# Post-norm attention and gated FFN layer on one core: the count of wide weights one block later, and the output normalisations of blocks 12 and 13 in other places

## The chip, the cores and the metric

The kernel runs on one core of a Trainium2 chip. A core has five engines that work side by side, each through its own queue in order: TensorE (PE, with its weight loads as PEld) does the matrix products, VectorE (DVE) and ScalarE (ACT) work on elements, GpSimd (POOL) does element work on SBUF, and SyncE (SP) issues most transfers. Products go to PSUM, which this kernel uses as eight banks of 128 x 512 float32. The metric is the time on the device in microseconds (us), the median over runs; lower is better.

## The reference

The input `x` has 4 x 2048 tokens of 256 features. The layer is attention in chunks of 32 tokens, with a decay mask and no softmax, then a gated FFN whose weights are integers of -127 to 127 times 1/127; each is followed by a layer norm over the sum with its input.

```python
Q = x @ W_q.T ; K = x @ W_k.T ; V = x @ W_v.T
mask = where(diff >= 0, decay ** diff, 0)              # within chunks of 32 tokens
O = ((Q K^T) * mask) @ V                               # chunk by chunk
x = layernorm(x + sigmoid(x @ W_g.T) * O @ W_o.T + x)
h = silu(x @ wg.T) * (x @ wu.T)                        # 768 hidden features
x = layernorm(x + h @ wd.T)
```

## The kernel before

**Tiles and precision.** The 8192 tokens are 16 blocks of 512 (`NB`, numbered 0 to 15). A block is held either with tokens on partitions (four groups of 128 tokens, `NG`) or with features on partitions. The FFN's products are exact to about float32: the integer weights are stored as `hi` (fp32r) and `lo` (f16), and each activation is split in two likewise, as the rounded part `hi` and the rest `lo`. ScalarE's copy makes `u_hi` from `u` (L757), GpSimd subtracts to make `u_lo` (L758).

**Products of the FFN.** `ffn_up` (L722) goes over chunks of 128 hidden features, six (`KH`) to a block. A chunk takes two banks, `pg` for the gate and `pu` for the other factor, with eight products. Then ScalarE makes the Sigmoid `s` of `pg` (L741), VectorE multiplies `s` by `pg` (L743), which frees the gate's bank, then `pu` by `s` (L755), which frees the other. `ffn_down` (L764) multiplies the six `u_hi` and six `u_lo` by `fd` for each of the four token groups (`fdn`, L625; even groups take the `hi` parts first), and VectorE adds the residual (L772) and takes the moments (L307, L308).

**Attention of a block** has a scores product (`ps`, L578), masked by VectorE (L589), a values product (`po`, L599), multiplied by the gate to give `goT` (L606), and an output product. Most blocks do the products for v, y, the gate and the output by a scheme with seven half-size products (`seven`, L439), in two halves: the first four, then `others`. For block 15 `attn_out` (L640) does the output directly (`pa`) and a whole layer norm on VectorE and ScalarE.

**The main loop** (L834) runs over b = 0 to 13. Pass b does the FFN of block b, the attention of block n = b + 2 from its scores on, and the first attention products of m = b + 3, which exist (`more`) up to b = 12. Blocks 14 and 15 have their FFN after the loop (L913 on), interleaved, with block 15 in two halves of 256 columns.

**Layer norms in the loop** are spread: VectorE's moments, then a root on ScalarE (`root`, L311), a reciprocal on VectorE and three small operations on GpSimd (`scale_and_shift`, L348), and four scalings on ScalarE, one for each group (`normalize`, L361), after which the block is stored by SP (L784). The root needs another activation table than the Sigmoids; after the roots the loop executes a Sigmoid of one column (`table`, L885), so that the table for Sigmoids is loaded at that place.

**Order.** The program is laid out by a framework that may issue an instruction earlier than it is written, when it thinks its inputs ready, and that puts in the waits. `keep_in_program_order` pins an instruction behind the one written just before it on the same engine; `in_turn` does that always, `in_steady_turn` only while `steady` is true (L842, passes 1 to 12), `free` never. An instruction that isn't pinned may be placed ahead of a pinned one. The SP queue carries, in every pass, 16 transfers that finish the transposition of `h` (`move_h`, L683; `split_h`, L706, then makes `hT_hi` on ScalarE and `hT_lo` on GpSimd).

**The count of wide weights.** The exact scheme holds only for integers up to 128 in size. `look_up` (L260) takes the largest size in each of nine pieces of the weights on VectorE, five before the loop and four in pass 0, after the values. `count_wide` (L272), right behind it in pass 0, compares them (`wide`, L275), adds over partitions with a product by ones (`pw`, L279), and makes an integer on VectorE. It is read at the very end, where a block for wide weights runs if the count isn't zero.

**Around the change.** In pass b the scalings of block b - 2 (`r_before`) stand after the values. In pass 13 the root of block 12 stands after `split_h` of block 14, and behind `ffn_down` come the root of 13 and then, for blocks 12 and 13, `scale_and_shift`, four scalings and the store (L899 to L907). Then the FFN of 14 begins (L918).

Of the kernel before, what the change touches and what calls it, by code (L numbers as in the profile page):

```python
# [51 lines left out]
AF = mybir.ActivationFunctionType  # L52
ALU = mybir.AluOpType
# [5 lines left out]
TB = 512  # L59
NG = TB // P  # L60
# [11 lines left out]
def kernel(  # L72
# [187 lines left out]
    def look_up(which):  # L260
        pieces = [piece for pieces in ffn_int for piece in pieces]
        for i in which:
            reduced = nc.vector.tensor_reduce(
                top[:, i : i + 1],
                pieces[i].rearrange("p k n -> p (k n)"),
                mybir.AxisListType.X,
                ALU.max,
                apply_absolute_value=True,
            )
            tc.keep_in_program_order(reduced)  # L270

    def count_wide():  # L272

        wide = const.tile([P, top.shape[1]], F32, tag="wide", name="wide")
        nc.vector.tensor_scalar(wide, top, EXACT, None, ALU.is_gt)  # L275
        ones = const.tile([P, 1], F32, tag="ones", name="ones")
        nc.vector.memset(ones, 1.0)
        pw = bank("pw")
        nc.tensor.matmul(pw[:1, : top.shape[1]], lhsT=ones, rhs=wide, start=True, stop=True)  # L279
        count = const.tile([1, 1], F32, tag="count", name="count")  # L280
        nc.vector.tensor_reduce(count, pw[:1, : top.shape[1]], mybir.AxisListType.X, ALU.add)
        n_wide = const.tile([1, 1], I32, tag="n_wide", name="n_wide")
        nc.vector.tensor_copy(n_wide, count)
        return n_wide

    def in_turn(ins):
        tc.keep_in_program_order(ins)
# [70 lines left out]
        nc.gpsimd.tensor_tensor(shift, mv[:, :, 0], minus, ALU.mult)  # L358
        return scale, shift

    def normalize(r, scale, shift):  # L361
        for g in range(NG):
            in_turn(
                nc.scalar.activation(  # L364
                    r[:, g, :],
                    r[:, g, :],
                    AF.Identity,
                    bias=shift[:, g : g + 1],
                    scale=scale[:, g : g + 1],
                )  # L370
            )
# [137 lines left out]
    def split_y(b, x_sums):  # L509
        yT = work.tile([P, KD, TB], F32, tag="yT", name=f"yT_{b}")  # L510
        return yT, seven(f"y_{b}", feature_major(w_sums["m"], x_sums), by_features(yT))
# [125 lines left out]
    def flat(t, gs):  # L637
        return t[:, gs, :].rearrange("p g d -> p (g d)")

    def attn_out(b, goT, up=H_UP):  # L640
        xn = xns.pop(b)
        r = norm.tile([P, NG, D], F32, tag="h", name=f"h_{b}")

        def residual(gs, pb):
            nc.vector.tensor_tensor(flat(r, gs), pb, flat(xn, gs), ALU.add)

        project_back(b, (chunked(goT),), (chunked(wo),), residual, "pa")
        layer_norm(r, f"a{b}", on_r=HALF, on_dst=up)
        return r
# [69 lines left out]
        return hi, lo  # L719


    def ffn_up(b, hT, uT, chunks, cols=slice(0, TB), held=False):  # L722

        n = cols.stop - cols.start
        for hc in chunks:
            pg = bank(f"fg_{b}_{hc}_{cols.start}")[:, :n]
            pu = bank(f"fu_{b}_{hc}_{cols.start}")[:, :n]

            kinds = (0, 1) if hc % 2 == 0 else (1, 0)
            for kind in kinds:  # L730
                for pb, w in ((pg, fg), (pu, fu)):
                    for dc in range(KD):
                        nc.tensor.matmul(  # L733
                            pb,
                            lhsT=w[kind][:, dc, hc * P : (hc + 1) * P],
                            rhs=hT[kind][:, dc, cols],
                            start=(kind == kinds[0] and dc == 0),
                            stop=(kind == kinds[1] and dc == KD - 1),
                        )
            s = work.tile([P, n], F32, tag="s", name=f"s_{b}_{hc}")  # L740
            nc.scalar.activation(s, pg, AF.Sigmoid, scale=SCALE / H_UP)  # L741

            gated = nc.vector.scalar_tensor_tensor(  # L743
                s, pg, U_UP / H_UP**2, s, ALU.mult, ALU.mult
            )
            in_steady_turn(gated)
            if len(uT[0]) == hc:
                for kind, dtype, tiles in zip(("hi", "lo"), (F32R, F16), uT):
                    tiles.append(
                        acts.tile([P, TB], dtype, tag=f"u_{kind}", name=f"u_{kind}_{b}_{hc}")  # L750
                    )

            def multiply(hc=hc, pu=pu, s=s):
                u = work.tile([P, n], F32, tag="u", name=f"u_{b}_{hc}")
                in_steady_turn(nc.vector.tensor_tensor(u, pu, s, ALU.mult))  # L755
                hi, lo = uT[0][hc][:, cols], uT[1][hc][:, cols]
                nc.scalar.copy(hi, u)  # L757
                nc.gpsimd.tensor_tensor(lo, u, hi.bitcast(F32), ALU.subtract)  # L758

            if held:  # L760
                return multiply
            multiply()
# [68 lines left out]

    scales_h = scales_out = r_out = None
    table = const.tile([P, 1], F32, tag="table", name="table")
    for b in range(NB - 2):  # L834
        n = b + 2
        m = b + 3
        more = m < NB
        xns[n] = load_xn(n)
        hT = hTs.pop(b)
        uT = [], []  # L840
        yT, v, sg = ahead
        steady = 0 < b < NB - 3  # L842
        if b:
            normalize(hs[b + 1], *scales_h)
        moving = move_h(b + 1, hs[b + 1])
        ffn_up(b, hT, uT, range(0, 1))
        if b == 0:
            g_rest()
            x_sums = token_sums(xTs[m], f"x_{m}")
        ffn_up(b, hT, uT, range(1, 2))  # L850
        sT = attn_scores(n, yT)
        if m + 1 < NB:
            xTs[m + 1] = load_xT(m + 1)
        ffn_up(b, hT, uT, range(2, 3))
        if more:
            v_next, v_rest = split_v(m, x_sums)
        multiply = ffn_up(b, hT, uT, range(3, 4), held=True)
        if more:
            v_rest()
        multiply()  # L860
        goT = attn_values(n, sT, v, sg)
        if scales_out is not None:
            normalize(r_before, *scales_out)
            store(b - 2, r_before)
        if b == 0:
            look_up(range(5, n_pieces))
            n_wide = count_wide()
        if more:
            go_sums = token_sums(goT, f"go_{n}")
            y_next, y_rest = split_y(m, x_sums)  # L870
        ffn_up(b, hT, uT, range(4, KH))
        r_before = r_out
        if more:
            y_rest()
            sg_next, g_rest = split_gate(m, x_sums)
            hs[n], out_rest = split_out(n, go_sums)
            g_rest()
            mv_h = out_rest()
            ahead = y_next, v_next, sg_next
            hTs[b + 1] = split_h(b + 1, moving)  # L880
            std_h = root_in_turn(mv_h, of_h, f"h_{b}")
            if b:
                mv_before, std_before = mv_out, root_in_turn(mv_out, of_out, f"out_{b}")

            in_turn(nc.scalar.activation(table, eps, AF.Sigmoid))  # L885
            if m + 1 < NB:

                x_sums = token_sums(xTs[m + 1], f"x_{m + 1}", in_turn)

            def between():  # L890
                return scale_and_shift(mv_h, std_h, of_h, f"h_{b}")

            r_out, mv_out, scales_h = ffn_down(b, uT, hs.pop(b), between)
            if b:
                scales_out = scale_and_shift(mv_before, std_before, of_out, f"out_{b}")
        else:
            hs[n] = attn_out(n, goT, 1)
            hTs[b + 1] = split_h(b + 1, moving)
            mv_before, std_before = mv_out, root_in_turn(mv_out, of_out, f"out_{b}")  # L899
            r_out, mv_out, _ = ffn_down(b, uT, hs.pop(b))  # L900
            std = root_in_turn(mv_out, of_out, f"last_{b}")
            for block, r, mv, of_r in (
                (b - 1, r_before, mv_before, std_before),
                (b, r_out, mv_out, std),
            ):
                normalize(r, *scale_and_shift(mv, of_r, of_out, f"f{block}"))
                store(block, r)  # L907

# [4 lines left out]
    cols = [slice(i * per * P, (i + 1) * per * P) for i in range(2)]  # L915
    uT_last = [], []
    uT = [], []
    ffn_up(last - 1, hTs[last - 1], uT, half[0])  # L918
    hTs[last] = transpose_h(last, hs[last], 1)
    ffn_up(last - 1, hTs[last - 1], uT, half[1])  # L920
    early = half[0]
    ffn_up(last, hTs[last], uT_last, early, cols[0])
# [211 lines left out]
```

## Time and profile before

| | |
|---|---|
| median of 3 runs | 540.35 us (540.34 to 541.08) |
| profiled execution | 540.2 us |
| its span, first to last instruction | 538.4 us |
| mean granted TensorE clock | 0.986 |
| one pass of the loop, fdn to fdn (115.02 to 146.62) | 31.6 us |
| pass 13, fdn of 12 ends to fdn of 13 ends | 468.0 to 490.6 |
| last fdn product of block 15 ends | 529.2 |

All times in the text are of the profiled execution, counted from the start of its span, unless they are called a median. About 1.8 us of the profiled execution lie outside its span. "Granted clock" is the share of full speed at which TensorE was let run. A line of the chain of waits has a start, a length, and what ran; a line of waits names the waiting engine, tile and line, then what ended the wait, then the total, the number and the longest wait in us. In a line of the order of time, the text in brackets at the end is the idle time before it and what ended that. "xN" is a number of instructions. A line of a stretch has the stretch and its length, the busy time of PE, PEld, DVE, ACT and POOL with the number of instructions, the granted clock, the DMA engines' busy share and GB/s.

### The profile page before, as it was taken

What the parts mean: (1) busy time and instruction counts of PE and PEld (TensorE: products, weight loads), DVE (VectorE), ACT (ScalarE), POOL (GpSimd) and SP (SyncE); (2) the same over time, 40 slices, a digit from 0 to 9 for tenths busy, and PEclk for the clock granted to TensorE, in tenths of its full rate; (3) what the DMA queues carried; (4) which work ended last, traced back from release to release, by engine and by line L of the source; (5) the groups of instructions that cost most, each with busy time, mean ns of one, the idle gap of its engine ahead of it and who ended that gap; (6) DMA issues with size and microseconds to landing.
All of it is one profiled execution on the core that took longest, in us unless ns stands there. A gap on an engine that the chain in (4) does not pass through costs nothing.

```text
span 538.4 us, 10518 instructions
## 1 busy us (share of the span) xinstructions
PE 521.3 (97%) x3642; PEld 423.1 (79%) x3642; DVE 388.9 (72%) x979; ACT 320.3 (59%) x638; POOL 330.4 (61%) x450
## 2 busy tenths in 40 slices
PE   8999799999999999999999999999999999999793
PEld 5588678797878879787887978788897878877592
DVE  4679748678686867868676786867677686777684
ACT  2374436466665656566575656666565675757753
POOL 5231736684857768486676848667684766643553
PEclk9999979999999999999999999999999999999898
DMA  7631301211313132131312312131231312020102
GB/s 252 184 112 39 79 0 44 77 40 37 91 52 99 43 83 73 34 89 55 101 41 61 98 33 87 52 105 41 51 108 31 88 53 68 1 78 15 64 1 82
DMA packets 43176, 36.90 MB, mean 69 GB/s; under 512 B 4720, under 2 KB 39024, under 8 KB 43120
## 3 DMA queue, kind: packets, MB, share of 16 engines
q1 hardware_dynamic: 41712, 34.88, 22.1%
q10 hardware_dynamic: 1376, 1.31, 0.7%
q8 instruction: 30, 0.49, 0.4%
q14 instruction: 26, 0.21, 0.1%
q0 software_dynamic: 32, 0.00, 0.0%
HBM read 20.45 MB, written 8.39 MB: 54 GB/s over the span
## 4 chain that ended last, share of the span: by engine, by line
PE 95%; DVE 2%; ACT 2%; issue 0%
PE fg L733 16%; PE fu L733 16%; PE fdn L625 15%; PE p_y L409 8%; PE p_v L427 8%; PE p_g L409 8%; PE p_o L427 8%; PE po L599 5%; PE ps L578 3%; PE pa L625 2%; PE py L539 1%; PE pv L558 1%; PE pg L523 1%; PE pi L178 1%; ACT r L364 1%; PE fdn L977 1%
## 5 line engine op out<-in xcount | busy, mean ns | idle before, releaser
L758 POOL TENSOR_TENSOR u_lo<-u,u_hi 128x512 f16<-128x512 f32 (+1 forms) x102 | 123.6, 1214 | 128.8 <-ACT u_hi L757 126.9
L757 ACT CAST u_hi<-u 128x512 fp32r<-128x512 f32 (+1 forms) x102 | 60.6, 594 | 67.4 <-DVE u L755 67.1
L743 DVE SCALAR_TENSOR_TENSOR s<-fg,s 128x512 f32<-128x512 f32 (+1 forms) x102 | 66.7, 656 | 43.4 <-ACT s L741 43.4
L741 ACT ACTIVATE s<-fg 128x512 f32<-128x512 f32 (+1 forms) x102 | 56.7, 569 | 40.2 <-PE fg L733 40.0
L733 PE MATMUL fg<-hT_hi,fg_hi 128*128 128x512 f32 (+1 forms) x204 | 75.7, 453 | 2.8 <-DVE s L743 2.8
L755 DVE TENSOR_TENSOR u<-fu,s 128x512 f32<-128x512 f32 (+1 forms) x102 | 66.9, 658 | 10.7 <-POOL u_lo L758 1.1
L733 PE MATMUL fu<-hT_hi,fu_hi 128*128 128x512 f32 (+1 forms) x204 | 61.6, 383 | 0.0
L733 PE MATMUL fg<-hT_lo,fg_lo 128*128 128x512 f16 (+1 forms) x204 | 59.2, 372 | 0.0
L733 PE MATMUL fu<-hT_lo,fu_lo 128*128 128x512 f16 (+1 forms) x204 | 59.0, 371 | 0.0
L625 PE MATMUL fdn<-fd_hi,u_hi 128*128 128x256 f32 x360 | 52.9, 289 | 0.0
L733 PEld LDWEIGHTS fg<-hT_hi,fg_hi 128*128 128x128 f32 x204 | 36.1, 192 | 12.0 <-DVE s L743 3.2
L625 PEld LDWEIGHTS fdn<-fd_hi,u_hi 128*128 128x128 f32 x360 | 45.1, 189 | 0.4
L625 PE MATMUL fdn<-fd_lo,u_lo 128*128 128x256 f16 x360 | 44.6, 273 | 0.0
L733 PEld LDWEIGHTS fu<-hT_hi,fu_hi 128*128 128x128 f32 x204 | 37.8, 190 | 8.5 <-DVE s L743 0.3
L364 ACT ACTIVATE h<-h,shift_h,scale_h 128x256 f32<-128x256 f32 x52 | 27.0, 592 | 22.6 <-POOL shift_h L358 22.6
L733 PEld LDWEIGHTS <-fu_lo 128*128 128x128 f16 x204 | 20.0, 98 | 21.8 <-issue 0.6
L716 POOL TENSOR_TENSOR hT_lo<-hT,hT_hi 128x512 f16<-128x512 f32 x28 | 35.3, 1280 | 2.3 <-ACT hT_hi L715 2.3
L625 PEld LDWEIGHTS <-u_lo 128*128 128x128 f16 x360 | 32.7, 98 | 4.7 <-POOL u_lo L758 0.2
L772 DVE SCALAR_TENSOR_TENSOR r<-fdn,h 128x512 f32<-128x512 f32 x30 | 20.7, 691 | 20.4 <-PE fdn L625 20.4
L733 PEld LDWEIGHTS <-fg_lo 128*128 128x128 f16 x204 | 16.0, 99 | 20.7 <-issue 13.2
L599 PE MATMUL po<-sT,v 128*128 128x128 f32 x256 | 31.2, 275 | 0.0
L599 PEld LDWEIGHTS po<-sT,v 128*128 128x128 f32 x256 | 30.0, 192 | 0.6 <-issue 0.5
(192 smaller groups left out, 1134.4 us busy)
## 6 DMA issues: line engine op xcount, KB each, us to landing
x<-in_x_dram SPq DMA_DIRECT2D x16, 512.0 KB, 3.6
xT<-in_xT_dram SPq DMA_DIRECT2D x15, 512.0 KB, 4.3
hT<-sq SPq DMA_DIRECT2D x224, 32.0 KB, 1.9
out_dram<-r SPq DMA_DIRECT2D x14, 512.0 KB, 4.8
fg_int<-in_ffn_gT_dram SPq DMA_DIRECT2D x3, 256.0 KB, 8.3
fu_int<-in_ffn_uT_dram SPq DMA_DIRECT2D x3, 256.0 KB, 7.0
fd_int<-in_ffn_dT_dram SPq DMA_DIRECT2D x3, 256.0 KB, 6.0
out_dram<-r SPq DMA_DIRECT2D x6, 128.0 KB, 3.1
```

The source lines that it names most:

```text
L364: nc.scalar.activation(r[:, g, :], r[:, g, :], AF.Identity, bias=shift[:, g : g + 1], scale=scale[:, g : g + 1],)
L409: nc.tensor.matmul(pb, lhsT=a[i - 1], rhs=b[i - 1], start=first, stop=True, skip_group_check=True,)
L427: nc.tensor.matmul(pb[:, g * P : (g + 1) * P], lhsT=b[i - 1][:, g * P : (g + 1) * P], rhs=a[i - 1], start=first and g == 0, stop=True, ski ...
L599: nc.tensor.matmul(po[:, cols], lhsT=v[:, g, dc * P : (dc + 1) * P], rhs=sT[:, cols], start=True, stop=True,)
L625: nc.tensor.matmul(pb[:, j * D : (j + 1) * D], lhsT=part[:, g * P : (g + 1) * P], rhs=w, start=(i == 0), stop=(i == len(terms) - 1),)
L716: nc.gpsimd.tensor_tensor(in_order[1], whole, in_order[0].bitcast(F32), ALU.subtract)
L733: nc.tensor.matmul(pb, lhsT=w[kind][:, dc, hc * P : (hc + 1) * P], rhs=hT[kind][:, dc, cols], start=(kind == kinds[0] and dc == 0), stop=( ...
L741: nc.scalar.activation(s, pg, AF.Sigmoid, scale=SCALE / H_UP)
L743: gated = nc.vector.scalar_tensor_tensor(s, pg, U_UP / H_UP**2, s, ALU.mult, ALU.mult)
L755: in_steady_turn(nc.vector.tensor_tensor(u, pu, s, ALU.mult))
L757: nc.scalar.copy(hi, u)
L758: nc.gpsimd.tensor_tensor(lo, u, hi.bitcast(F32), ALU.subtract)
```

## The change

- `count_wide` is called in pass 1 instead of pass 0. `look_up` stays in pass 0.
- `steady` holds in pass 13 too, and ends after the loop; the residual of `attn_out` is added under `in_steady_turn`.
- In pass 13 the scalings of block 11 and its store stand between chunks 2 and 3 rather than after the values.
- In pass 13 the root of block 12, the return to the Sigmoids' table (now the function `back_to_sigmoids`) and `scale_and_shift` stand after the values, ahead of chunks 4 and 5; the scalings of 12 and its store stand after these chunks.
- The root of 13 stays behind `ffn_down`; the return to the Sigmoids' table follows it. Its scalings move into the FFN of block 14, two groups after chunk 1 and two after the transposition of block 15. The first Sigmoid of block 14 is pinned.

```diff
-    def normalize(r, scale, shift):
-        for g in range(NG):
+    def normalize(r, scale, shift, groups=range(NG)):
+        for g in groups:
...
-            nc.vector.tensor_tensor(flat(r, gs), pb, flat(xn, gs), ALU.add)
+            in_steady_turn(nc.vector.tensor_tensor(flat(r, gs), pb, flat(xn, gs), ALU.add))
...
-    def ffn_up(b, hT, uT, chunks, cols=slice(0, TB), held=False):
+    def ffn_up(b, hT, uT, chunks, cols=slice(0, TB), held=False, order=free):
...
-            nc.scalar.activation(s, pg, AF.Sigmoid, scale=SCALE / H_UP)
+            order(nc.scalar.activation(s, pg, AF.Sigmoid, scale=SCALE / H_UP))
...
+    def back_to_sigmoids():
+
+        in_turn(nc.scalar.activation(table, eps, AF.Sigmoid))
+
...
-        steady = 0 < b < NB - 3
+        steady = b > 0
...
         ffn_up(b, hT, uT, range(2, 3))
+        if not more:
+            normalize(r_before, *scales_out)
+            store(b - 2, r_before)
...
-        if scales_out is not None:
+        if scales_out is not None and more:
             normalize(r_before, *scales_out)
             store(b - 2, r_before)
         if b == 0:
             look_up(range(5, n_pieces))
+        if b == 1:
             n_wide = count_wide()
         if more:
             go_sums = token_sums(goT, f"go_{n}")
             y_next, y_rest = split_y(m, x_sums)
+        else:
+            std_out = root_in_turn(mv_out, of_out, f"out_{b}")
+            back_to_sigmoids()
+            scales_out = scale_and_shift(mv_out, std_out, of_out, f"out_{b}")
         ffn_up(b, hT, uT, range(4, KH))
...
-            in_turn(nc.scalar.activation(table, eps, AF.Sigmoid))
+            back_to_sigmoids()
...
         else:
+            normalize(r_before, *scales_out)
+            store(b - 1, r_before)
             hs[n] = attn_out(n, goT, 1)
             hTs[b + 1] = split_h(b + 1, moving)
-            mv_before, std_before = mv_out, root_in_turn(mv_out, of_out, f"out_{b}")
             r_out, mv_out, _ = ffn_down(b, uT, hs.pop(b))
-            std = root_in_turn(mv_out, of_out, f"last_{b}")
-            for block, r, mv, of_r in (
-                (b - 1, r_before, mv_before, std_before),
-                (b, r_out, mv_out, std),
-            ):
-                normalize(r, *scale_and_shift(mv, of_r, of_out, f"f{block}"))
-                store(block, r)
+            std_out = root_in_turn(mv_out, of_out, f"last_{b}")
+            back_to_sigmoids()
+            scales_out = scale_and_shift(mv_out, std_out, of_out, f"last_{b}")
+    steady = False
...
-    ffn_up(last - 1, hTs[last - 1], uT, half[0])
+    ffn_up(last - 1, hTs[last - 1], uT, range(0, 1), order=in_turn)
+    ffn_up(last - 1, hTs[last - 1], uT, range(1, 2))
+    normalize(r_out, *scales_out, range(0, NG // 2))
+    ffn_up(last - 1, hTs[last - 1], uT, range(2, KH // 2))
     hTs[last] = transpose_h(last, hs[last], 1)
+    normalize(r_out, *scales_out, range(NG // 2, NG))
+    store(last - 2, r_out)
     ffn_up(last - 1, hTs[last - 1], uT, half[1])
```

## The prediction

> **What bounds the kernel now.** I read the page first, for shares and clock, then TensorE's own waits, then the chain of waits around the two long ones, then ScalarE's order of time in the last three blocks.
>
> ```profile
> PE 521.3 (97%) x3642; PEld 423.1 (79%) x3642; DVE 388.9 (72%) x979; ACT 320.3 (59%) x638; POOL 330.4 (61%) x450
> ```
>
> ```profile
> PE pw L279 <- DVE wide L275: 3.6, 1, 3.6
> PE fg L733 <- DVE s L743: 2.8, 1, 2.8
> PE pi L178 <- DVE idle L175: 1.5, 1, 1.5
> ```
>
> TensorE is busy 97% and waits only three times worth listing: in the count of wide weights (block 0), before a gate product in block 14, and at the very start. Everything between is TensorE back to back, so a microsecond counts only if it removes or adds TensorE idle time or lowers its clock. The chain around the first wait, and then the same place one block later:
>
> ```profile
> 62.26 1.80 PE po L599 x16
> ...
> 64.78 2.38 DVE top L263 x4
> 67.16 0.02 issue
> 67.18 0.36 DVE wide L275
> 67.54 0.14 issue
> 67.67 0.20 PE pw L279 x2
> 67.88 3.71 PE p_y L409 x8
> ...
> 100.46 1.79 PE po L599 x16
> 102.25 1.73 PE p_y L409 x8
> ```
>
> TensorE stands still while VectorE does four maxima (2.38 us) and the comparison, and afterwards the eight y products take 3.71 us instead of 1.73. The stretches show why, and the same behind the second wait (time, busy time of five engines, granted clock, DMA):
>
> ```profile
> 66.00:67.00 1.00, 0.00 (x0) 0.00 (x0) 1.00 (x2) 0.00 (x0) 0.92 (x3) 0.70 0.95 358
> ...
> 503.00:504.00 1.00, 1.00 (x4) 0.35 (x3) 1.00 (x3) 1.00 (x3) 0.47 (x1) 0.66 0.00 0
> 506.00:507.00 1.00, 1.00 (x4) 0.76 (x4) 0.98 (x2) 0.58 (x2) 0.04 (x1) 0.64 0.00 0
> ```
>
> The clock falls to half at 66.40 (0.4 us at full, 0.6 at half give 0.70) and returns near 73.24; it falls at 503.32 and returns at 506.72. Last, ScalarE at the end:
>
> ```profile
> 484.30 0.62 ACT L757 CAST u_hi<-u 128x512 fp32r<-128x512 f32 x1 [0.80 <-DVE u L755]
> 484.94 1.28 ACT L316 ACT_TABLE_LOAD   x1
> ...
> 492.22 0.60 ACT L741 ACTIVATE s<-fg 128x512 f32<-128x512 f32 x1 [2.00 <-PE fg L733]
> 492.83 1.28 ACT L316 ACT_TABLE_LOAD   x1
> 494.13 0.30 ACT L316 ACTIVATE rstd_last<-mv_f,eps 128x4 f32<-128x4 f32 x1
> 494.41 4.05 ACT L364 ACTIVATE r<-r,shift_f,scale_f 128x256 f32<-128x256 f32 x8
> 498.37 0.60 ACT L757 CAST u_hi<-u 128x512 fp32r<-128x512 f32 x1
> 498.99 1.28 ACT L741 ACT_TABLE_LOAD   x1
> 500.28 1.08 ACT L741 ACTIVATE s<-fg 128x512 f32<-128x512 f32 x2
> ```
>
> Eight scalings and two table loads keep the second Sigmoid of block 14 back until 500.28, so PSUM banks come free late and chunk 4 starts at 501.66 instead of 498.9.
>
> **What the Trainium skill says.** "TensorE: Matmul & The Clock Gate", Part 1, has the clock gate judged by a free-running window of 3413 ns, with half rate after an idle one. The trace agrees on the length: 503.32 - 66.40 = 436.92 us is 128.0 windows, and the cold stretches are two (6.84) and one (3.40). It is stricter here: the window 499.91 to 503.32 was idle for 1.75 us (until 501.66) and was throttled, the one before it with 1.0 us idle was not. "ScalarE: Activation LUTs", What ACT_TABLE_LOAD costs, gives about 1283 ns plus a drain of 1380 ns for a switch. The trace has the 1.28 us, but the next activation starts 1.29 us after the load does (498.99 to 500.28), so I price a switch at 1.29.
>
> **The count, moved to block 1.** From the start of po to the start of fdn, block 0 takes 62.26 to 83.43 = 21.17 us, block 1 takes 100.46 to 115.02 = 14.56. The difference, 6.61, is the wait with pw (5.62 against 1.79 = 3.83) and the cold clock (67.88 to 83.43 = 15.55 against 12.77 = 2.78). What is late next in block 0 is VectorE: the maxima stay and end at 67.16, then the two y sums (0.42 each) end near 68.0. TensorE would do the first y products (1.54) and two chunks (3.8) from 64.05 and want these sums from about 69.4 to 70.2 on. Cover of over 1.4 us, so no wait; without it a microsecond would cost a microsecond. In block 1 the comparison reads maxima long finished and is free to go into an idle gap; pw costs TensorE 0.14 to 0.20. The y sum of block 1 is pinned behind the cast of the count, 0.15 + 0.14 us of VectorE in front of a 0.24 us gap: nothing seen by TensorE, 1.3 us if the comparison isn't placed ahead and pw waits for it. Net -6.45.
>
> **Block 14.** The eight scalings of 12 and 13 leave their place: 12's go to block 13, 13's follow the Sigmoids in two halves of about 1.0 us. The new order is root of 13 (waits for fdn's last moments), table back, Sigmoid 0 pinned behind it. From the end of fdn(13): residual and moments 2.0, root 0.3, load 1.28, small activation 0.2, Sigmoid 0.6, its VectorE products 1.4: 5.75 us, while chunk 3 wants those banks 6.3 to 6.75 after fdn's end. It fits with 0.5 to 1 us to spare. So the wait of 2.76 goes, and the cold clock: chunks 4, 5 and the three halves run 501.66 to 509.79 = 8.13 against 2 x 1.82 + (509.79 - 507.15) = 6.28, so 1.85. Together -4.6. POOL's six u_lo (1.28 each) keep pace with the 1.8 us chunks. The output store of 12 comes some 9 us earlier on SP; its queue is held by 16 transposing DMAs until 481.6 in any case, and nothing reads these stores before the second-next r2 tile.
>
> **Block 13, the price.** ScalarE gets into this 22.6 us block four scalings of 12 (2.05), a Sqrt for 12 (0.3) with two loads (2.56) and the small activation (0.2); the scalings of 11 (2.05) move ahead of values. By hand, in before's clock: Sigmoid 3 at 476.0, the cast of chunk 2 to 477.6 (VectorE in order now, as in block 12), scalings of 11 to 479.6, cast 3 to 480.2, load, Sqrt to 481.75, load, small activation to 483.3, Sigmoids 4 and 5 to 484.4. Behind them VectorE, in order: reciprocal of 12 (waits for the Sqrt), then s4, u4, s5, u5 = 4 x 0.66, to 486.5; cast 5 ends at 487.2 where it ended at 484.92. Queued behind u5 is also the attention residual, so the moments of 15 come at 489.6 instead of 487.2. TensorE's first fdn group wants cast 5 at 485.75: idle about 1.5; POOL's u_lo of 4 and 5 (1.28 each) end at 488.5, wanted at 487.9: another 0.65. Sum +2.15. The h chain runs in parallel: scalings of 12 to 489.2, load 490.5, root, two casts to 491.9, hT_lo on POOL to 493.9; with fdn ending at 492.8 the first f16 products want it at 493.75 to 493.97. Just covered; it holds the same 2.15 in place should fdn wait less.
> Bounds: below, 0, if both Sigmoids are issued ahead of the Sqrt; above, 4.0, if the scalings of 11 go ahead of Sigmoid 3 (all of the chain 2 us later, and goT too). I take 2.15, since cast 3 and the Sqrt stand earlier in the program than the Sigmoids and are ready when ScalarE comes free; Sigmoid 3 preceded cast 2 before.
> Clock: 2.15 us idle lie within 485.6 to 488.6, so most positions of the window hold over 1.5 of it. Between 1.0 (spared) and 1.75 (throttled) the trace decides nothing. A window at half rate costs 1.7. I take it as a little likelier than not: +1.7, bounds 0 and 3.4.
>
> **Sum.** 6.45 + 4.6 - 2.15 - 1.7 = 7.2. Profiled span 538.4 to 531.2; with the 1.8 us outside it 533.0. Its execution was 540.2, the median 540.35, so 533.1.
>
> **Rivals.** (1) The same with the clock staying full: 531.4. For it: the idle time is in three pieces with products between. Against: 1.75 sufficed. (2) Sigmoids 4 and 5 slip ahead of the Sqrt, fdn waits at most 1 us: 529.3 to 530.3. For: they are free to be placed anywhere. Against: the order argument above. (3) The scalings of 11 ahead of Sigmoid 3: 540.35 - 11.05 + 4.0 + 1.7 to 3.4 = 535.0 to 536.7. For: they are ready early; against: Sigmoid 3's product was ready at 475.99, before cast 2 could run at 476.4. (4) Slower: ScalarE's queue in block 13 also takes free Sigmoids between the two table switches, each such place a pair of loads more, 2.6 us. With (3)'s 4.0, two such pairs (5.2) and two cold windows (3.4) it is 540.35 - 11.05 + 12.6 = 541.9. It decides once the last cast of block 13 is some 9 us later than before; for it, block 14 of before does take a free Sigmoid between two Sqrts (492.22); against, the Sigmoids of 13 are ready within 3 us of each other. (5) The count's wait only moves to block 1, 1.3 us of it: 534.4, within the range.
>
> **Chances.** Forecast 0.38, (1) 0.26, (2) 0.15, (3) and (5) 0.17, (4) 0.04. The range 529.9 to 535.9 leaves out part of (2), part of (3), and (4), about 0.2. A measurement of this kernel tells 0.2% (1.1 us) from no change: faster 0.94, within 0.02, slower 0.04.
>
> **What would show it.** Right: no wait of TensorE at pw, y products of block 0 at 1.7 us for eight, full clock near 70; none for VectorE's s in block 14; a new wait at fdn in block 13 released by ScalarE's cast, some 1.5 us, and one by POOL's u_lo; two table loads between cast 3 and Sigmoid 4. Wrong: a wait at chunk 4 of 14 still there, pw waiting in block 1, fdn of 13 without a wait, or Sigmoid 3 behind the scalings of 11.

## The result, and the profile after

| | before | after |
|---|---|---|
| median of 4 runs each, same chip | 540.42 us (540.34 to 541.08) | 533.5 us (532.54 to 534.39) |
| ratio, 95% interval | 1 | 0.9869 (0.985 to 0.9888) |
| span of the profiled execution | 538.4 us | 532.6 us |
| mean granted clock | 0.986 | 0.993 |

The changed kernel is 1.3% faster, and the predicted 533.1 us lies 0.4 from the median. The profiled execution of the changed kernel was the slowest of its four (534.39 us), so places are compared by stretches within one trace and not by their distance from the start. The page's first line, and TensorE's waits:

```profile
PE 519.3 (98%) x3642; PEld 421.4 (79%) x3642; DVE 389.6 (73%) x979; ACT 320.0 (60%) x640; POOL 330.1 (62%) x450
```

```profile
...
PE fdn L625 <- POOL u_lo L758: 0.7, 2, 0.4
PE fg L733 <- DVE s L743: 0.5, 1, 0.5
PE fdn L625 <- ACT u_hi L757: 0.4, 1, 0.4
PE fg L733 <- POOL hT_lo L716: 0.4, 1, 0.4
```

The two long waits (3.6 and 2.8 us) are gone. In their place stand five short ones, 2.0 us together, all in blocks 13 and 14. The chain of waits around the count, block 0 and then block 1 (start, length, what ran):

```profile
62.86 1.79 PE po L599 x16
64.65 1.73 PE p_y L409 x8
...
77.41 5.43 PE fdn L625 x48
...
94.44 1.79 PE po L599 x16
96.22 0.13 PE pw L279 x2
96.35 1.92 PE p_y L409 x8
...
109.32 2.72 PE fdn L625 x24
```

The y products follow po at once in block 0 and take 1.73 us instead of 3.71. In block 1, pw costs its 0.13 us, with no wait ahead of it. From po to fdn block 0 now takes 77.41 - 62.86 = 14.55 us, and block 1 takes 14.88. The stretches at the old place of the first cold clock and at the new short waits (the column after the five engines is the granted clock):

```profile
70.00:71.00 1.00, 1.00 (x6) 0.88 (x5) 0.82 (x2) 0.94 (x3) 0.27 (x1) 1.00 0.00 0
...
481.00:482.00 1.00, 0.55 (x5) 0.42 (x5) 1.00 (x3) 1.00 (x3) 0.87 (x2) 1.00 0.02 8
482.00:483.00 1.00, 0.59 (x7) 0.29 (x5) 1.00 (x6) 1.00 (x3) 0.81 (x1) 1.00 0.00 0
```

The clock is full at 70, and it stays full where TensorE stands idle for 0.45 and 0.41 us within two. In this trace it falls only at 524.99, behind the last product. ScalarE's order of time in block 13 and the start of 14:

```profile
473.63 0.60 ACT L757 CAST u_hi<-u 128x512 fp32r<-128x512 f32 x1
474.25 1.28 ACT L316 ACT_TABLE_LOAD   x1
475.54 0.30 ACT L316 ACTIVATE rstd_out<-mv_f,eps 128x4 f32<-128x4 f32 x1
475.86 1.28 ACT L837 ACT_TABLE_LOAD   x1
477.15 0.20 ACT L837 ACTIVATE table<-eps 128x1 f32<-128x1 f32 x1
477.26 1.07 ACT L741 ACTIVATE s<-fg 128x512 f32<-128x512 f32 x2
...
480.84 0.62 ACT L757 CAST u_hi<-u 128x512 fp32r<-128x512 f32 x1 [0.80 <-DVE u L755]
481.37 2.07 ACT L364 ACTIVATE r<-r,shift_out,scale_out 128x256 f32<-128x256 f32 x4
483.46 1.28 ACT L316 ACT_TABLE_LOAD   x1
484.75 0.30 ACT L316 ACTIVATE rstd_a<-mv_a,eps 128x4 f32<-128x4 f32 x1
```

Both table loads stand between the cast of chunk 3 and the Sigmoids of chunks 4 and 5, and the four scalings of block 12 and the load for block 15's root stand ahead of the two casts of block 14's `h`. What this does to TensorE:

```profile
479.26 1.80 PE L625 MATMUL fdn<-fd_hi,u_hi 128*128 128x256 f32 x10
481.51 0.38 PE L625 MATMUL fdn<-fd_hi,u_hi 128*128 128x256 f32 x1 [0.45 <-ACT u_hi L757]
...
482.87 0.94 PE L625 MATMUL fdn<-fd_lo,u_lo 128*128 128x256 f16 x7 [0.41 <-POOL u_lo L758]
...
488.21 0.38 PE L733 MATMUL fg<-hT_lo,fg_lo 128*128 128x512 f16 x1 [0.39 <-POOL hT_lo L716]
...
493.99 0.59 PE L733 MATMUL fg<-hT_lo,fg_lo 128*128 128x512 f16 x2 [0.50 <-DVE s L743]
```

TensorE works through ten products of fdn ahead of the one that needs the late cast, so it waits for it in small pieces. The last line is the wait that remains in block 14, where before had 2.76 us. The two waits at fdn are listed with 0.86 us; from the start of its first product to the end of its last, fdn of block 13 takes 1.57 us longer than before (7.40 against 5.83), so the list shows only part of what the stops cost.

### The profile page after: what moved, and what is told of

Same layout as the page of the kernel before. It is cut to its first block, busy times and chain, and to the rows that moved or that the text cites. A ratio compares the mean times of both kernels' runs of the same rounds, so it can differ in the third digit from the quotient of the medians.

```text
span 532.6 us, 10517 instructions
## 1 busy us (share of the span) xinstructions
PE 519.3 (98%) x3642; PEld 421.4 (79%) x3642; DVE 389.6 (73%) x979; ACT 320.0 (60%) x640; POOL 330.1 (62%) x450
## 4 chain that ended last, share of the span: by engine, by line
PE 91%; DVE 4%; ACT 3%; POOL 1%; issue 0%; DVEq 0%; POOLq 0%
PE fg L733 15%; PE fu L733 14%; PE fdn L625 14%; PE p_v L427 8%; PE p_y L409 8%; PE p_g L409 8%; PE p_o L427 8%; PE po L599 5%; PE ps L578 3%; PE pg L523 1%; PE pa L625 1%; PE py L539 1%; PE pv L558 1%; DVE u L755 1%; POOL u_lo L758 1%; PE pi L178 1%
## 5 line engine op out<-in xcount | busy, mean ns | idle before, releaser
L758 POOL TENSOR_TENSOR u_lo<-u,u_hi 128x512 f16<-128x512 f32 (+1 forms) x102 | 123.5, 1213 | 125.9 <-ACT u_hi L757 123.6
L733 PE MATMUL fg<-hT_hi,fg_hi 128*128 128x512 f32 (+1 forms) x204 | 74.9, 447 | 0.0
L733 PE MATMUL fu<-hT_hi,fu_hi 128*128 128x512 f32 (+1 forms) x204 | 61.3, 381 | 0.1
L733 PE MATMUL fg<-hT_lo,fg_lo 128*128 128x512 f16 (+1 forms) x204 | 59.0, 369 | 0.9 <-DVE s L743 0.5
L733 PE MATMUL fu<-hT_lo,fu_lo 128*128 128x512 f16 (+1 forms) x204 | 58.1, 366 | 0.0
L733 PEld LDWEIGHTS fu<-hT_hi,fu_hi 128*128 128x128 f32 x204 | 37.5, 188 | 8.4 <-DVE u L755 0.4
L733 PEld LDWEIGHTS fg<-hT_hi,fg_hi 128*128 128x128 f32 x204 | 35.7, 189 | 8.6
L733 PEld LDWEIGHTS <-fu_lo 128*128 128x128 f16 x204 | 19.8, 98 | 22.2 <-issue 0.9
L733 PEld LDWEIGHTS <-fg_lo 128*128 128x128 f16 x204 | 15.9, 98 | 20.8 <-issue 13.0
## 6 DMA issues: line engine op xcount, KB each, us to landing
out_dram<-r SPq DMA_DIRECT2D x6, 128.0 KB, 3.4
```

The source lines that it names most:

```text
L733: nc.tensor.matmul(pb, lhsT=w[kind][:, dc, hc * P : (hc + 1) * P], rhs=hT[kind][:, dc, cols], start=(kind == kinds[0] and dc == 0), stop=( ...
```

## The experiments

To compare the end of the kernel I use three landmarks of TensorE's order of time: the first fdn product of block 13, the `pt` product that begins the transposition of block 15, in the middle of block 14's FFN, and the first fdn product of block 15. The "stretch" is the first to the last.

| kernel | median us (interval of runs where it matters) | ratio (95%) | fdn13 to pt + pt to fdn15 | stretch |
|---|---|---|---|---|
| before | 540.42 | | 11.09 + 27.54 | 38.63 |
| changed | 533.5 | 0.9869 (0.985 to 0.9888) | 13.19 + 24.92 | 38.11 |
| count only | 533.93 | 0.9887 (0.9873 to 0.9902) | 11.09 + 27.48 | 38.57 |
| normalisations only | 539.67 | 0.9997 (0.9988 to 1.0006) | 13.19 + 24.96 | 38.15 |
| filled wait | 537.45 | 0.9962 (0.995 to 0.9974) | 11.10 + 27.51 | 38.61 |
| 13's scalings late | 532.67 | 0.9868 (0.9854 to 0.9882) | 13.21 + 24.50 | 37.71 |
| 12's scalings late | 533.08 | 0.9873 (0.9855 to 0.989) | 12.68 + 24.49 | 37.17 |
| 15's norm last | 531.41 | 0.9843 (0.9827 to 0.9859) | 12.68 + 23.58 | 36.26 |
| 12's root back | 531.94 | 0.9855 (0.9839 to 0.9871) | 11.09 + 25.39 | 36.48 |
| the last two together | 530.65 (529.75 to 530.96) | 0.9827 (0.9812 to 0.9842) | 11.10 + 24.35 | 35.45 |
| and 12's scalings behind its root | 529.19 (528.82 to 529.77) | 0.9811 (0.9788 to 0.9834) | 11.09 + 23.85 | 34.94 |
| and 15's norm in parts | 530.59 (529.23 to 531.12) | 0.9833 (0.9808 to 0.9858) | 11.09 + 23.71 | 34.80 |
| changed, run again | 533.14 (532.66 to 533.89) | 0.9887 (0.9866 to 0.9908) | 13.21 + 24.96 | 38.17 |

The runs are from several chips; each ratio is to the kernel before, measured beside that run on the same chip. In kernels that add a line above them, line numbers are one or a few higher (L734 for L733, L759 for L758).

### The two halves of the change

The count alone, on the kernel before:

```diff
             look_up(range(5, n_pieces))
+        if b == 1:
             n_wide = count_wide()
```

> The kernel before with only the count moved to pass 1. Theory (the count's wait and the half clock behind it are the larger part): 540.4 less 6.3, 534.1 us, with the 2.8 us wait in block 14 still there. Rival (part of the wait comes back in pass 1, because the y sums of VectorE stand behind the count's cast): 535.4 or more, with a wait of TensorE at pw or at the y products near 96 us.

The normalisations alone, on the changed kernel:

```diff
             look_up(range(5, n_pieces))
-        if b == 1:
             n_wide = count_wide()
```

> The changed kernel with the count back in pass 0: only the normalisations are moved. Theory (the 4.6 us saved in block 14 are nearly given back by new waits in blocks 13 and 14, 1.6 at fdn, 0.5 at hT_lo, 0.7 at chunk 3 and 1.4 behind it): about 540.4 less 0.5, 539.9 us. Rival (the moves are worth their saving less only the waits of block 13): 540.4 less 2.4, 538.0 us or less.

The count alone gives 0.9887, that is -6.1 us (-6.9 to -5.3); the normalisations alone give 0.9997, -0.2 us, with zero inside the interval (-0.6 to +0.3). So all of the gain that can be measured is the count, and the prediction's -0.75 from the three terms of blocks 13 and 14 (-4.6, +2.15, +1.7) was not there as a time; their stretch is 0.48 us shorter.

The run with the count alone holds a second answer. It still has the wait of block 14, and its clock does not fall. Its waits, and one stretch within the wait and one behind it:

```profile
PE fg L733 <- DVE s L743: 2.7, 1, 2.7
...
PE fdn L625 <- ACT u_hi L757: 0.7, 1, 0.7
PE fdn L625 <- POOL u_lo L758: 0.4, 1, 0.4
```

```profile
494.00:495.00 1.00, 0.00 (x0) 0.00 (x0) 0.00 (x0) 0.99 (x3) 0.50 (x1) 1.00 0.94 347
...
497.00:498.00 1.00, 1.00 (x6) 0.51 (x6) 1.00 (x2) 0.98 (x2) 0.28 (x1) 1.00 0.00 0
```

With the same wait and the clock full the stretch takes 38.57 us, against 38.63 with one window at half rate. From `pt` to the first fdn of block 14 it does gain 1.50 us (12.23 against 13.73), but from there to the first fdn of block 15 it needs 1.44 us more (15.25 against 13.81), with two waits at fdn of block 14 (0.67 and 0.41) that before does not have: behind the wait ScalarE, VectorE and GpSimd turn products into `u_hi` and `u_lo`, and TensorE arrives there before them. The 1.85 us that the prediction put on this clock were worth nothing.

### The clock without the move

Before the count, in block 0 of the kernel before, three products of zeros fill part of the wait, and the maxima, the wait for them and pw stay where they are:

```diff
+            pf = bank("pf")
+            for _ in range(3):
+                in_turn(nc.tensor.matmul(pf, lhsT=idle[:, :P], rhs=idle, start=True, stop=True))
             n_wide = count_wide()
```

> The kernel before with three products of zeros added on TensorE ahead of the count's product in pass 0, pinned behind the values: about 2.8 us of work inside the 3.6 us wait. Theory (2.8 of the 6.6 us lost there are the half clock): the wait stays, the clock doesn't fall, 540.4 less 2.7, 537.7 us. Rival (the slow y products come from banks or from their sums, not from the clock): no change or up to 0.5 us slower.

The chain of waits of this run around the count, and the stretch at 66:

```profile
62.34 1.80 PE po L599 x16
...
64.86 2.38 DVE top L263 x4
...
67.76 0.20 PE pw L279 x2
67.95 1.92 PE p_y L409 x8
...
80.91 5.43 PE fdn L625 x48
```

```profile
66.00:67.00 1.00, 0.71 (x2) 0.00 (x0) 1.00 (x3) 0.00 (x0) 0.92 (x3) 1.00 0.93 358
```

The maxima still lead to pw, but the y products take 1.92 us instead of 3.71, and the stretch from po to fdn is 80.91 - 62.34 = 18.57 against 21.17: -2.60 where the prediction's cold clock was 2.78. By the ratio it is -2.05 us (-2.7 to -1.4). A wait of 1.0 us at pw stays. So the count's gain is made of two parts, and the clock's is shown apart from the wait's. In block 14 of this run the clock did fall behind the wait, at half rate from 500.2 to 503.6, and the stretch is 38.61, as in before (38.63) and as with the clock full (38.57).

### Block 14: what stands ahead of the Sigmoids

All four scalings of block 13 behind the last chunks of block 14:

```diff
-    normalize(r_out, *scales_out, range(0, NG // 2))
...
-    normalize(r_out, *scales_out, range(NG // 2, NG))
-    store(last - 2, r_out)
     ffn_up(last - 1, hTs[last - 1], uT, half[1])
+    normalize(r_out, *scales_out)
+    store(last - 2, r_out)
```

> The changed kernel with all four scalings of block 13 and its store behind chunk 5 of block 14. Theory (these scalings stand ahead of the Sigmoid of chunk 2 on ScalarE, and the late u_lo of chunk 5 holds fdn of 14 up): 533.5 less about 1.4, 532.1 us, with the wait of fdn for u_lo in block 14 gone. Rival (the hold-up comes from the late Sigmoid 0 and the moments behind it, the scalings lie in idle time): no change, 533.5 us.

Behind `pt` the stretch is 0.42 us shorter (24.50 against 24.92), and the interval of the ratio cannot be told from the changed kernel's. The scalings between the Sigmoids are a small part of what block 14 lost; that they were the main part (1.4 us expected) is refuted, and the wait of fdn for `u_lo` in block 14 is still there (0.40).

VectorE's order of time in the changed kernel shows the other part:

```profile
486.99 2.29 DVE L331 TENSOR_SCALAR h<-h,mv_a,rstd_a 128x256 f32<-128x256 f32 x4
489.20 0.68 DVE L772 SCALAR_TENSOR_TENSOR r<-fdn,h 128x512 f32<-128x512 f32 x1
489.91 0.75 DVE L307 BATCH_NORM_STATS2 st_f<-r 128x6 f32<-128x256 f32 x2
490.58 0.30 DVE L308 BATCH_NORM_AGGREGATE mv_f<-st_f 128x2 f32<-128x6 f32 x2
```

Four operations of block 15's attention norm run ahead of block 13's second residual, though fdn has ended near 486.7. The last moments are there at 490.88, 4.2 us after fdn's end instead of the 2.0 that the prediction counted, and the root, the table and the first Sigmoid of block 14 all stand behind them. The trace of before had the same order, with the last moments at 493.65, 2.85 us after the end of fdn's last product at 490.80:

```profile
489.83 2.09 DVE L331 TENSOR_SCALAR h<-h,mv_a,rstd_a 128x256 f32<-128x256 f32 x4
492.00 0.65 DVE L772 SCALAR_TENSOR_TENSOR r<-fdn,h 128x512 f32<-128x512 f32 x1
```

So the next kernel, made from the one with 13's scalings late, puts block 15's norm behind the residual (`norm_now=False` leaves it out of `attn_out`):

```diff
-            hs[n] = attn_out(n, goT, 1)
+            hs[n] = attn_out(n, goT, 1, norm_now=False)
...
             r_out, mv_out, _ = ffn_down(b, uT, hs.pop(b))
+            layer_norm(hs[n], f"a{n}", on_r=HALF, on_dst=1)
```

> The run with the late scalings of 13, and the layer norm of block 15 written behind the FFN's down product of 13 (its moments and scalings on VectorE behind the residuals of 13, its root beside that of 13). Theory (the 2.3 us of VectorE's scalings of 15 lie ahead of the second residual of 13 and so hold Sigmoid 0 of block 14 back; the root of 15 holds hT back): the waits at chunk 3 (0.5) and at hT_lo (0.4) of block 14 go, from the fdn of 13 to the fdn of 15 it takes 36.5 us instead of 37.7, the time is near 531.5 us. Rival (the transposition of 15 then comes late and takes the same time back): 532.7 us, unchanged.

Behind `pt` 0.92 us go (24.50 to 23.58), and ahead of it 0.53 (13.21 to 12.68), since the load and root of block 15 no longer stand ahead of the casts of block 14's `h`, and TensorE doesn't wait for hT_lo. The median follows: 531.41, ratio 0.9843. The wait at chunk 3 does not go, it is 0.3 us. The last moments of 13 are now there 2.0 us after fdn's end (489.54 and 487.55), as the prediction had counted. But the moments and the root of 15 still stand ahead of the root of 13, which starts at 491.09, 3.5 us after fdn's end, where the kernel with only 13's scalings late has 4.3 (491.44 and 487.19).

### Block 13: what the root of 12 costs

The root of block 12 goes back behind the casts of block 14's `h`, where it shares the table load of 15's root, so that its own pair of table loads is gone; the scalings of 12 leave block 13 (made from the kernel with 13's scalings late):

```diff
-        else:
-            std_out = root_in_turn(mv_out, of_out, f"out_{b}")
-            back_to_sigmoids()
-            scales_out = scale_and_shift(mv_out, std_out, of_out, f"out_{b}")
...
-            normalize(r_before, *scales_out)
-            store(b - 1, r_before)
             hTs[b + 1] = split_h(b + 1, moving)
+            mv_before, std_before = mv_out, root_in_turn(mv_out, of_out, f"out_{b}")
...
             back_to_sigmoids()
+            scales_before = scale_and_shift(mv_before, std_before, of_out, f"out_{b}")
...
     hTs[last] = transpose_h(last, hs[last], 1)
+    normalize(r_before, *scales_before)
+    store(last - 3, r_before)
```

> The run with the late scalings of 13, and block 12's root put back beside the roots of 15 and 13, its four scalings behind the transposition of block 15; so block 13 has neither a second pair of table loads nor these scalings. Theory (the table loads and scalings of 12 cost TensorE 1.6 us at fdn and 0.5 us at hT_lo): both waits go, fdn of 13 to fdn of 15 takes 35.6 us instead of 37.7, the time is near 530.6 us. Rival (the scalings of 12 cost the same again in block 14): 532.7 us, unchanged.

And with the root left where the change has it, only the scalings of 12 and the store moved behind the transposition of block 15:

```diff
-            normalize(r_before, *scales_out)
-            store(b - 1, r_before)
+            scales_before = scales_out
...
     hTs[last] = transpose_h(last, hs[last], 1)
+    normalize(r_before, *scales_before)
+    store(last - 3, r_before)
```

> The run with the late scalings of 13, and only the four scalings of block 12 moved into block 14; the root of 12 with its two table loads stays ahead of chunks 4 and 5 of block 13. Theory (the table loads alone delay the casts that fdn waits for, the scalings only hT): the fdn waits stay (about 0.4 each for u_hi and u_lo), the wait at hT_lo goes, 37.2 us for the stretch, near 532.2 us. Rival (the scalings are the delay): the fdn waits go, near 530.6 us.

The two runs split the price of block 13. Moving only the scalings takes 13.21 to 12.68: 0.53 go, at hT_lo, and the waits at fdn stay. Of TensorE's waits in that run the one for hT_lo is the one that is gone. The same 0.53 went when the load and root of 15 left that place, so they belong to the queue of both ahead of the casts of `h`, and taking either away is enough. Moving the root of 12 as well takes it to 11.09, the value of before: the root with its two loads costs 1.59, at fdn. The second removal gives back 0.90 behind `pt` (24.49 to 25.39). The scalings of 12 stand in block 14 in both runs, and beside the early root they cost nothing there (24.50 and 24.49). With the root moved, ScalarE does all four in one row (494.61 to 496.68), ahead of the cast of chunk 2 and two Sigmoids; that this row is the cause was not tried by itself.

### Versions put together

Both last edits at once, the norm of 15 last and the root of 12 back:

> Both edits of the two runs before together. Theory: the gains add, fdn of 13 to fdn of 15 takes 34.9 us, the time is near 529.9 us. Rival (one chain of ScalarE, VectorE and GpSimd bounds block 14 in any order): not under 35.6 us for that stretch, 530.6 us.

The stretch is 35.45 us, below either alone (36.26 and 36.48). The two gains, 1.45 and 1.23, would add to 35.03, so they add only in part. From there, the scalings of 12 go right behind its root in block 13, where ScalarE has time while fdn runs:

```diff
             hTs[b + 1] = split_h(b + 1, moving)
-            mv_before, std_before = mv_out, root_in_turn(mv_out, of_out, f"out_{b}")
+            std_out = root_in_turn(mv_out, of_out, f"out_{b}")
+            normalize(r_before, *scale_and_shift(mv_out, std_out, of_out, f"out_{b}"))
+            store(b - 1, r_before)
...
-            scales_before = scale_and_shift(mv_before, std_before, of_out, f"out_{b}")
...
-    normalize(r_before, *scales_before)
-    store(last - 3, r_before)
```

> The run with both edits, and the four scalings of block 12 placed right behind its root in block 13, into the time in which ScalarE waits for the moments of 13. Theory (these scalings still delay block 14 by 0.8 us where they stood): fdn of 13 to fdn of 15 takes 34.7 us instead of 35.4, the time is near 530.0 us. Rival (block 14 is bound by the late Sigmoid 0 alone): 35.4 us and 530.7 us.

ScalarE's order of time in block 13 of this kernel, and TensorE's waits:

```profile
479.09 1.28 ACT L316 ACT_TABLE_LOAD   x1
480.38 0.30 ACT L316 ACTIVATE rstd_out<-mv_f,eps 128x4 f32<-128x4 f32 x1
482.43 2.08 ACT L364 ACTIVATE r<-r,shift_out,scale_out 128x256 f32<-128x256 f32 x4 [1.75 <-POOL shift_out L358]
487.94 0.30 ACT L316 ACTIVATE rstd_a<-mv_a,eps 128x4 f32<-128x4 f32 x1 [3.43 <-DVE mv_a L308]
488.14 0.28 ACT L316 ACTIVATE rstd_last<-mv_f,eps 128x4 f32<-128x4 f32 x1
488.44 1.28 ACT L838 ACT_TABLE_LOAD   x1
```

```profile
...
PE fdn L625 <- POOL u_lo L759: 0.4, 1, 0.4
PE fg L734 <- DVE s L744: 0.3, 1, 0.3
```

One load serves the three roots of 12, 15 and 13 and one leads back, and the scalings of 12 lie in a gap of ScalarE behind the casts that fdn and `h` need. The move is worth 0.51 of stretch where 0.8 was thought. This is the fastest kernel run: 529.19 us, ratio 0.9811, and 4.0 us below the changed kernel run beside it on the same chip (533.14), where the intervals of the runs don't meet. Of that 3.2 us are the stretch (38.17 to 34.94); the rest lies outside it.

Last, only part of block 15's norm is held back; its moments and root stand ahead of fdn:

```diff
+            mv_a = moments(hs[n], f"a{n}", order=in_turn)
+            rstd_a = root(mv_a, f"a{n}", HALF, order=in_turn)
             r_out, mv_out, _ = ffn_down(b, uT, hs.pop(b))
-            layer_norm(hs[n], f"a{n}", on_r=HALF, on_dst=1)
+            layer_norm_rest(hs[n], mv_a, rstd_a, HALF, 1)
```

> The run before, and the moments and the root of block 15 put ahead of the down product of 13, so that only the reciprocal and the scalings of 15 stand behind it. Theory (root of 13 then comes 1.3 us earlier): the wait of 0.3 us at chunk 3 goes, 34.3 us for the stretch, near 529.6 us. Rival (VectorE puts the scalings of 15 ahead of the second residual again, as in the changed kernel): no better than the run before, 530.0 us or slower.

VectorE's order of time in this kernel:

```profile
484.81 1.10 DVE L334 TENSOR_SCALAR h<-h,mv_a,rstd_a 128x256 f32<-128x256 f32 x3
485.83 0.68 DVE L776 SCALAR_TENSOR_TENSOR r<-fdn,h 128x512 f32<-128x512 f32 x1
```

Three of the four scalings, which aren't pinned, were placed ahead of the second residual after all. The root of 13 still came 1.3 us earlier (2.2 us after fdn's end instead of 3.6) and the wait at chunk 3 went, as the theory had it, but the stretch is 34.80: 0.14 shorter than the version above, and no faster in time (the intervals of the runs overlap). So an earlier first Sigmoid of block 14 is worth little by now. The changed kernel was run again beside them:

> The changed kernel itself, beside the two others on one chip. Expected: its ratio to before as first measured, 0.987, and the stretch from fdn of 13 to fdn of 15 at 38.1 us.

Both came as expected: 0.9887, with 0.987 inside its interval, and 38.17 us.

## Why the prediction came out right, and where it did not

- **Count, block 0: right.** 6.61 predicted, 21.17 - 14.55 = 6.62 measured; no wait for the y sums. The two parts in it are confirmed separately by the filled wait (2.60 for the clock).
- **Count, block 1: right in kind.** 0.14 to 0.20 predicted, 14.88 - 14.56 = 0.32 measured: pw's 0.13, and 1.92 instead of 1.73 for the y products behind it, which the estimate left out. Net -6.30 against -6.45, and -6.1 by the ratio of the count alone.
- **Block 13, idle time: right in sum, not in place.** +2.15 predicted and 13.19 - 11.09 = +2.10 measured. ScalarE's order is the predicted one, and the last cast ended at 481.46, or 487.2 in before's clock (fdn of 13 started 5.71 earlier in the trace of after), as computed. But TensorE did the products of other groups first, and so lost 1.6 us at fdn and not 2.15; the other 0.5 came from hT_lo, which the prediction had as just covered. The two partial moves show 1.59 for the root with its loads and 0.53 at hT_lo.
- **Block 13, clock: wrong.** +1.7 predicted as a little likelier than not, 0 measured: the clock stayed full. The prediction wanted over 1.5 us of idle time in one window of the clock. The waits at fdn came to 0.45 and 0.41, so no window could hold more than 0.86 of them, less than the 1.0 that was spared in before. The prediction had named the full clock as its first rival; that it is the pieces, and not the small sum, that saved the clock isn't shown.
- **Block 14: wrong by 2.0 us, the step that failed.** -4.6 predicted, 24.92 - 27.54 = -2.62 measured. The wait of 2.76 went, leaving 0.50 at chunk 3. Two terms were mis-sized. "Residual and moments 2.0", in a sum whose terms add to 5.78 and not 5.75, was 4.2, since VectorE put four operations of block 15's norm ahead of the second residual; before's own trace, with 2.85, could have warned of it. Holding the norm back gave 0.92 of stretch behind `pt`. And "the cold clock, 1.85", more than the 1.7 that the prediction itself gives a window at half rate, was worth nothing here: with the wait in place the stretch is 38.57 at full clock and 38.61 and 38.63 with a window at half rate, because ScalarE, VectorE and GpSimd set the pace behind it. The missing 1.85 and the 0.50 left over are 0.37 more than the miss; where that came back was not followed.
- **The sum.** -6.30 + 2.10 + 0 - 2.62 = -6.8, against -7.2 predicted and -6.9 between the medians. The total is near partly because two errors of about 2 us, a clock that did not fall and a gain that wasn't there, have opposite signs; that part is luck. As a time, the moves of the normalisations are worth nothing that these runs can measure.
- **Still open.** The 0.42 us of the late scalings are below what these runs can tell as a time; they are a reading of the traces alone. How the rest of block 14's loss divides between the first Sigmoid's delay and the casts behind it was not separated.

## What to carry to other kernels

A wait of the busiest engine for a value that is only read at the end is removed by asking for it later, and here it was worth the wait plus the slow clock behind it; that was nearly all of this change. A slow clock may be priced at its lost cycles only where no other chain of engines is as late as TensorE (here 2.60 of 2.78 us in block 0, and nothing in block 14); the check is a run that has the same wait with the clock full. And when normalisations are moved away from the place that waits for ScalarE, look also at what VectorE may place ahead of the moments that the whole chain begins with: here three roots behind one table load, and the norm of the next block behind the residual, gave 3.2 us of stretch more than the change (4.0 between the medians).

## What the hardware showed that was not expected

- **The same wait falls on the clock or doesn't.** A wait of 2.7 us in block 14 brought half rate in before and in the run with the filled wait, and none in the run with the count alone. "TensorE: Matmul & The Clock Gate", Part 1, has the window run freely; the two falls in before, 436.92 us or 128.0 windows apart, agree with that, and so the position of a wait in its window could decide. The traces allow a rough check: in all of them the clock's changes lie whole numbers of such windows apart, so one change places all the windows. In the run with the count alone the clock falls only once, at 528.27, when the products are done:

```profile
528.00:529.00 1.00, 0.00 (x0) 0.00 (x0) 0.00 (x0) 0.00 (x0) 0.00 (x0) 0.63 0.41 142
```

Ten windows of 3.413 us earlier, at 494.13, a window begins in the middle of its wait (493.11 to 495.85) and holds 1.71 us of it. In before the window from 499.90 on holds 1.76 of the wait, in the run with the filled wait the one from 496.73 to 500.15 holds 2.38 (the wait is 496.38 to 499.12). So before and the count alone lie within 0.05 us of each other, and one lost the clock and the other did not. If the position decides, the limit lies between 1.71 and 1.76 us of idle time, by one trace on either side. It is then not the limit for a clock that is already slow: in block 0 of before the window from 66.40 on, itself at half rate, holds only 1.27 us of the wait, and the one behind it was at half rate too. That the position is the cause was not tried by itself.
- **The start varies between runs.** The first eight gate products (`pg`, L523) in the chain of waits of before and of the run with 15's norm last:

```profile
5.17 3.46 PE pg L523 x8
```

```profile
5.24 4.84 PE pg L523 x8
```

The code there is the same in both; in the changed kernel they took 4.00. The clock fits this: its records begin with a rise to full rate, at 4.97 in before, 6.17 in the changed kernel and 7.62 in the run with 15's norm last (the views count the time ahead of that as full), and in that last run the products start 0.85 to 1.02 us apart before the rise and 0.43 apart behind it. This alone moves a span by 1.4 us.

- **The end varies too.** From the first fdn of block 15 to the end of the span the changed kernel took 15.26 us in its first trace and 13.76 in its second. In between the traces agree: from the first `pv` product (L558), right behind those gate products, to the first fdn of block 13 all kernels with the count moved take 470.19 to 470.33 us. So differences below about 1 us were read from stretches that begin and end inside the trace.
